# A graph layer on one core: the values' projection put behind the key-value sums, norms moved to ScalarE, tiles packed to 125 columns

## The chip, the cores and the metric

The kernel runs on one core of a Trainium2 chip. A core has TensorE (matrix products; PE in the profile, PEld for the loading of its stationary operands), VectorE (DVE), ScalarE (ACT), GpSimd (POOL) and SyncE (SP), which here only issues transfers. Times are device microseconds (us) of a whole execution; a kernel's time is the median of its runs. The profile is of one execution, and its times count from the start of the profiled span.

## The reference

A graph of N = 3125 nodes with C = 256 features and 53125 edges (src, dst, weight), sorted by dst. All in f32:

```
xn  = layernorm(x)
Q, K = elu(xn Wq) + 1, elu(xn Wk) + 1      # 8 heads of 32
v   = (xn Wv) / N
KV  = sum over nodes of K (x) v, per head  # 32x32 each
Z   = 1 / (Q . sum of K + 1e-6), per node and head
msg = layernorm((Q KV Z N) Wm) g1 + b1
msg = layernorm(relu([xn, msg] W1) W2) g2 + b2
x   = x + (segment sum of weight * xn[src] by dst) W.T + b + xn + msg
x   = x + two best of 16 experts of layernorm(x), softmax weights
```

The attention is linear, so its sums over all nodes (KV and the sum of K) must be complete before the first query can be used.

## The kernel before

The nodes lie in 25 tiles of V = 125 rows; in SBUF a tile is padded to P = 128. Four stages follow each other.

**Projections and sums (0 to 111 us).** For each tile t, `normed` makes xn (L416, on VectorE), turns it with two transposes (L428) and copies the turned tile into xnT (L429). `projected` multiplies by W and Wk at once (L437, 512 columns) and by Wv (L439, 256 columns); ScalarE makes exp and relu of the keys (L441, L443), copies v with its factor 1/N (L447), copies y = xn W.T (L448) and replaces x by x + xn (L454); VectorE ends the keys (L445, k_sb). `summed`, issued one tile later, adds K^T v and, with a column of ones behind each half of v, K^T 1 into one PSUM bank pkv (L461, 129 columns for each of two halves). The means, variances and the chain of 13 small operations that finds 1/sqrt (`moments`, `rsqrt`) are made for BATCHES of tiles; AHEAD says at which tile a batch's statistics are asked for.

**The edge lists.** In the same time VectorE makes the edge lists in pieces (`windows`): a search for the row of dst in which each group of 5 nodes starts (cmp_h, row_f, row_i, L248 to L253), five gathers of those rows on GpSimd (L257), in them the place of the first edge (cmp_r and its sum, L267 to L272), five gathers of windows of 128 edges (L273), and then keys and weights from these (src_f, L286, and the operations over 640 elements that follow). The table first_d of the starts is stored on SP's queue after the last of them. LISTS says at which tile how many pieces are asked for. From tile HOT = 18 on, two `adjacency` blocks go along with each tile: VectorE spells out one-hot matrices (L335, L340), TensorE multiplies them (L355), ScalarE copies, SP stores.

**Groups of queries (122 to 556 us).** `asked` makes Q of a group of 3 or 4 tiles (L477, L483), the denominators (L489, one product of all columns with the sum of K spread over each head's 32 columns), and their reciprocals on all 128 partitions (L493 to L495). `mixer` multiplies by kvw, which is KV times Wm (L641), and does the two-layer network (L662, L673). The next group's `asked` is interleaved with it, and adjacencies and first messages (L625) with both, by the numbers in `groups`. Between the sums and the first group stand the mask that cuts KV to its heads, its transposes (L533), its product with Wm (L538), sixteen one-column products for a bias (L544), and a loop for edges that fit no window, which these inputs never enter (L559).

**Messages to 708 us, then the experts.** All messages are products of 128 x 128 adjacency blocks with y of a tile.

The instructions of each engine stand in an order that a planner has chosen when the program was built, from its own costs and from "issue after" notes; on an engine they run strictly in that order, so an instruction that waits holds up all behind it.

Of the kernel before, what the change touches and what calls it, by code (L numbers as in the profile page):

```python
# [17 lines left out]
N = 3125  # L18
# [35 lines left out]
BATCHES = ((0, 2), (2, 5), (5, 12), (12, 25))  # L54

LISTS = {1: 1, 6: 1, 7: 2, 8: 2, 14: 1, 15: 1, 16: 1}
AHEAD = {1: (2, 5), 2: (5, 9), 3: (9, 12), 4: (12, 15), 6: (15, 17), 9: (17, 21), 10: (21, 25)}
HOT = 18
# [4 lines left out]
def tile_gps_layer(ctx: ExitStack, tc: tile.TileContext, a: dict, out: bass.AP):  # L63
# [7 lines left out]
    y_d = dram.tile([NT * P, C], F32, name="y_d")  # L71
# [12 lines left out]
    def rsqrt(var, n, with_last=False):  # L84

        v = small.tile([P, 13], F32, name="rs_v")[:, :n]
        hv = small.tile([P, 13], F32, name="rs_h")[:, :n]
        bits = small.tile([P, 13], I32, name="rs_b")[:, :n]
        y = small.tile([P, 13], F32, name="rs_y")[:, :n]
        s = small.tile([P, 13], F32, name="rs_s")[:, :n]  # L90
# [10 lines left out]
    def stats(mv, src):  # L101
        st = small.tile([P, 6], F32, name="bn_st")
        nc.vector.bn_stats(st, src)
        return nc.vector.bn_aggr(mv, st)
# [58 lines left out]
    wcat = w_mix.tile([128, 2, 3 * C], F32, name="wcat")  # L163
    load_x(nc.sync, *LOADS[0])
    nc.scalar.dma_start(dst_0, a["dst"].rearrange("(p j) -> p j", p=V)[:, 0:1])
    for i, name in enumerate(("gnn_WT", "Wk", "Wv")):
        nc.scalar.dma_start(wcat[:, :, i * C : (i + 1) * C], a[name].rearrange("(k p) o -> p k o", p=128))
    load_x(nc.sync, *LOADS[1])
    wq = w_mix.tile([128, 2, C], F32, name="wq")
    wm = w_mix.tile([128, 2, C], F32, name="wm")  # L170
    w1 = w_mix.tile([128, 4, F], F32, name="w1")
    w2 = w_mix.tile([128, 4, C], F32, name="w2")

    def load_later(t):

        if t in (0, 1):
            load_x(nc.sync, *LOADS[4 + t])
        if t in (11, 13, 15, 17):
            w, name = ((wm, "Wm"), (wq, "Wq"), (w1, "W1"), (w2, "W2"))[(t - 11) // 2]
            nc.sync.dma_start(w, a[name].rearrange("(k p) o -> p k o", p=128))  # L180
        if t == 19:


            nc.sync.dma_start(out[N:, :].rearrange("(p r) (k c) -> p (r k) c", r=2, k=2),
                              ones[:, None, :].to_broadcast([LANES, 4, P]))
# [11 lines left out]
    xnT = w_mix.tile([128, 2, NT * P], F32, name="xnT")  # L197
# [11 lines left out]
    kv_bd = w_mix.tile([128, 2, 128], F32, name="kv_bd")  # L209
# [9 lines left out]
    def bank_a(of=4 * P):  # L219
        return adj_ps.tile([128, 512], F32, name="pa")[:, :of].rearrange("p (i e) -> p i e", e=of // 4)  # L220

# [7 lines left out]
    def windows():  # L229
# [11 lines left out]
        busy(16)  # L241
# [138 lines left out]
    pkv = kv_ps.tile([128, 2, 129], F32, name="pkv")  # L380
# [3 lines left out]
    v_ring = [w_mix.tile([P, 2, 129], F32, name=f"v_sb{i}") for i in range(3)]  # L384
    for v_sb in v_ring:
        nc.vector.memset(v_sb[:, :, 128:129], 1.0)
# [22 lines left out]
    def normed(t):  # L409

        nonlocal rstd, r0
        for t0, t1 in BATCHES:
            if t == t0:
                rstd, r0 = ready.pop(t0), t0
        xn = work.tile([P, C], F32, name="xn", bufs=4)
        ins = nc.vector.tensor_scalar(xn, x_all[:, t, :], mv[:, t, 0:1], rstd[:, t - r0 : t - r0 + 1],  # L416
                                      op0=ALU.subtract, op1=ALU.mult)
        with tc.issue_after(ins.ins):
            for batch in BATCHES:
                if t == batch[0]:  # L420
                    factors(*batch, rstd)
# [4 lines left out]
        ptr = a_ps.tile([128, 2, P], F32, name="tok", bufs=3)  # L426
        for k in range(2):
            nc.tensor.transpose(ptr[:, k, :], xn[:, k * 128 : (k + 1) * 128], ident)  # L428
        nc.scalar.copy(xnT[:, :, t * P : (t + 1) * P], ptr)  # L429

    def projected(t):

        cols = slice(t * P, (t + 1) * P)
        pyk = a_ps.tile([P, 2 * C], F32, name="big")
        pv = a_ps.tile([P, C], F32, name="tok", bufs=3)
        for k in range(2):
            nc.tensor.matmul(pyk, lhsT=xnT[:, k, cols], rhs=wcat[:, k, : 2 * C], start=(k == 0), stop=(k == 1))  # L437
        for k in range(2):
            last = nc.tensor.matmul(pv, lhsT=xnT[:, k, cols], rhs=wcat[:, k, 2 * C :], start=(k == 0), stop=(k == 1))  # L439
        ek = work.tile([P, C], F32, name="ek", bufs=2)  # L440
        nc.scalar.activation(ek, pyk[:, C:], AF.Exp)  # L441
        k_sb = work.tile([P, C], F32, name="k_sb")
# [3 lines left out]
        v_sb = v_ring[t % 3]  # L446
        v_copy = nc.scalar.activation(v_sb[:, :, :128], pv.rearrange("p (c v) -> p c v", c=2), AF.Copy, scale=1.0 / N)  # L447
        nc.scalar.copy(y_of(t), pyk[:, :C])  # L448
        stored = nc.sync.dma_start(y_d[t * P : (t + 1) * P, :], y_of(t))
# [3 lines left out]
        with tc.issue_after(v_copy.ins):  # L453
            nc.scalar.activation(x_all[:, t, :], x_all[:, t, :], AF.Identity, scale=by[:, t : t + 1],  # L454
                                 bias=less[:, t : t + 1])
        return last, k_sb, v_sb

    def summed(t, k_sb, v_sb):
        for c in range(2):

            nc.tensor.matmul(pkv[:, c, :], lhsT=k_sb[:V, c * 128 : (c + 1) * 128], rhs=v_sb[:V, c, :],  # L461
                             start=(t == 0 and c == 0), stop=(t == NT - 1), skip_group_check=True)

    groups = ((4, 5, 0), (4, 23, 5), (4, 23, 7), (4, 23, 7), (3, 23, 7), (3, 23, 7), (3, 23, 2))
# [3 lines left out]
    def asked(t0, nt):  # L468

        w = nt * P  # L470
        c0 = t0 * P
        qT = mix.tile([128, 2, GROUP * P], F32, name="qT")
        asked_for.append(qT)
        for c in range(2):
# [9 lines left out]
            yield  # L484

# [5 lines left out]
        for part in (slice(0, 2 * P), slice(2 * P, w)):  # L491
# [6 lines left out]
    queries = [asked(sum(g[0] for g in groups[:i]), g[0]) for i, g in enumerate(groups)]  # L498
    rstd, r0 = None, 0
    kept = None  # L500
    normed(0)
    for t in range(NT):
# [8 lines left out]
        if t + 1 < NT:  # L511
            normed(t + 1)
# [13 lines left out]
    nc.vector.tensor_tensor(ksum, same_head[:, None, :].to_broadcast(shape), pkv[:, :, 128:129].to_broadcast(shape),  # L526
                            op=ALU.mult)
    nc.vector.tensor_tensor(kv_bd, same_head[:, None, :].to_broadcast(shape), pkv[:, :, :128], op=ALU.mult)
    for _ in range(2):
        next(queries[0])  # L530
    ptr = a_ps.tile([128, 2, 128], F32, name="tok", bufs=3)
    for c in range(2):
        nc.tensor.transpose(ptr[:, c, :], kv_bd[:, c, :], ident)  # L533
    kvT = work.tile([128, 2, 128], F32, name="msgT", bufs=1)
    nc.scalar.copy(kvT, ptr)
    for c in range(2):
        pw = a_ps.tile([P, C], F32, name="tok", bufs=3)
# [3 lines left out]
    pb1 = a_ps.tile([P, C], F32, name="tok", bufs=3)[:, :4]  # L541
# [17 lines left out]
    with tc.If(n_loops > 0):  # L559
        with tc.For_i(0, n_loops, 1) as it:  # L560
# [20 lines left out]
            nc.vector.scalar_tensor_tensor(t_d, t_d, float(P), p_d, op0=ALU.mult, op1=ALU.add)  # L581
# [9 lines left out]
            for t in range(NT):  # L591
                one = sel.tile([V, P], F32, name="l_one")
                nc.vector.tensor_scalar(one, iota_p[:V, :], p_s, took, op0=ALU.is_equal, op1=ALU.mult)
                pg = a_ps.tile([P, C], F32, name="tok", bufs=3)
# [7 lines left out]
    b_ps = ps.enter_context(tc.tile_pool(name="b_ps", bufs=1, space=PSUM))  # L602

# [9 lines left out]
    def messages(part, t, n, alone=False):  # L613
# [3 lines left out]
        if alone:  # L617
            pb = bank_a(2 * C)[:P].rearrange("p (a b) c -> p a (b c)", a=2)
        else:
            pb = b_ps.tile([P, 2, C], F32, name="pb")  # L620
        for i in range(n):
            rows = neighbours(part, t + i)
            for k in range(t0, t1):

                nc.tensor.matmul(pb[:, i, :], lhsT=rows[:, k - t0, :], rhs=y_of(k),  # L625
                                 start=(k == t0 and i == 0), stop=(k == t1 - 1), skip_group_check=True)
        nc.vector.tensor_tensor(x_all[:, t : t + n, :], x_all[:, t : t + n, :], pb[:, :n, :], op=ALU.add)  # L627
# [3 lines left out]
    def mixer(t0, nt, qT, following):  # L631

        w = nt * P
        c0 = t0 * P
        mv = small.tile([P, GROUP, 2], F32, name="mv_m")
        mw = mix.tile([P, GROUP, C], F32, name="mw")
# [655 lines left out]
```

## Time and profile before

| | |
|---|---|
| median of 3 runs | 1038.11 us (1036.63 to 1038.35) |
| the profiled execution | 1038.03 us, its span 1036.2 us |
| TensorE busy | 1007.1 us (97%), 6006 instructions |
| VectorE busy | 655.3 us (63%) |
| ScalarE, GpSimd busy | 263.9 us, 216.1 us |
| sum of tile 9 starts | 48.30 us |
| last sum ends, first group starts, second group starts | 110.9, 121.81, 152.86 us |
| last gather of edge windows issued, followed by the next waiting transfer | 34.18, 42.14 us |

In a line of the timeline stand: start, duration, engine, line, operation, output and inputs, tile, how many instructions were merged, and in brackets the idle time before it with what ended it. A product in f32 is two instructions, each of which runs over all columns. In a line of the stretches stand the stretch, its length, busy time and number of instructions of each engine, the granted clock of TensorE (1.00 is full speed), the share of the transfer engines in use and GB/s. A group's line has the busy time and the mean duration of one, then the engine's idle time before them and what ended it.

### The profile page before, as it was taken

How to read it: one execution, taken by the hardware profiler on the slowest of the kernel's cores; microseconds unless marked ns; L12 is line 12 of the kernel's file. 1: busy time of each engine (PE TensorE's matmuls, PEld its weight loads, DVE VectorE, ACT ScalarE, POOL GpSimd, SP SyncE). 2: the span in 40 equal slices, each digit the busy share in tenths (PEclk: the TensorE clock that was granted, in tenths of full speed). 3: DMA queues.
4: the chain of work that ended last, by engine and by line, in shares of the span. 5: the costliest groups of instructions: out<-in, count | busy, mean ns of one | idle time of the engine just before them, and what ended most of it. 6: DMA issues, size and time to landing. Idle time of an engine off the chain costs nothing.

```text
span 1036.2 us, 16279 instructions
## 1 busy us (share of the span) xinstructions
PE 1007.1 (97%) x6006; PEld 809.3 (78%) x6006; DVE 655.3 (63%) x1750; ACT 263.9 (25%) x577; POOL 216.1 (21%) x200
## 2 busy tenths in 40 slices
PE   7999999999999999999999999999999999999995
PEld 5667666686786887887877888887888888888884
DVE  8968699889787897956598148786932222222221
ACT  3666424323323233222141000103111111111110
POOL 3420100023100000000000001014445444545442
PEclk9999999999999999999999999999999999999998
DMA  6444104343344344553354455565757757667662
GB/s 214 95 131 145 53 31 167 128 140 136 122 137 138 133 162 133 175 181 143 140 182 155 159 167 166 183 194 179 209 155 226 240 170 234 199 202 225 206 189 26
DMA packets 70374, 165.09 MB, mean 159 GB/s; under 512 B 11091, under 2 KB 29934, under 8 KB 66314
## 3 DMA queue, kind: packets, MB, share of 16 engines
q1 hardware_dynamic: 53816, 138.10, 38.9%
q0 software_dynamic: 15520, 25.04, 10.7%
q8 instruction: 50, 0.82, 0.3%
q10 hardware_dynamic: 946, 0.79, 0.2%
q14 instruction: 42, 0.34, 0.1%
HBM read 105.85 MB, written 58.00 MB: 158 GB/s over the span
## 4 chain that ended last, share of the span: by engine, by line
PE 71%; DVE 10%; issue 1%; POOL 0%; ACT 0%; POOLq 0%; DVEq 0%; ACTq 0%
PE ph L1001 18%; PE pb L625 13%; PE po L1027 10%; PE po L738 8%; PE pa L355 6%; PE big L662 6%; PE tok L673 3%; DVE wone L340 2%; PE ptr L987 1%; PE pa L625 1%; PE big L477 1%; DVE one L335 1%; PE ph L799 1%; DVE wone L350 1%; PE big L489 1%
## 5 line engine op out<-in xcount | busy, mean ns | idle before, releaser
L1001 PE MATMUL ph<-xTb,wt 128*128 128x256 f32 (+2 forms) x992 | 204.5, 355 | 0.8 <-issue 0.8
L1001 PEld LDWEIGHTS ph<-xTb,wt 128*128 128x128 f32 x992 | 171.5, 190 | 24.9 <-ACT xTb L990 4.5
L625 PE MATMUL pb<-y_early,nbr 128*128 128x256 f32 x736 | 170.7, 382 | 0.4 <-DVE x_all L627 0.4
L340 DVE TENSOR_TENSOR wone<-one,wgts 128x1536 bf16<-128x1536 bf16 x150 | 140.6, 949 | 27.0 <-PE pa L355 26.8
L625 PEld LDWEIGHTS pb<-y_early,nbr 128*128 128x128 f32 x736 | 135.4, 190 | 17.2 <-DVE x_all L627 1.0
L355 PEld LDWEIGHTS <-one 128*128 128x128 bf16 x1875 | 117.3, 97 | 39.1 <-issue 19.1
L358 ACT COPY adj<-pa 128x512 f32<-128x512 f32 (+1 forms) x157 | 91.8, 586 | 194.2 <-PE pa L355 156.4
L355 PE MATMUL pa<-wone,one 128*128 128x128 bf16 x1875 | 130.3, 218 | 2.3 <-DVE wone L340 0.9
L1008 DVE TENSOR_TENSOR hid<-hid,ph 128x512 f32<-128x512 f32 (+2 forms) x62 | 38.3, 618 | 145.7 <-PE ph L1001 135.4
L1027 PE MATMUL po<-wt,hid 128*128 128x256 f32 (+1 forms) x456 | 115.2, 385 | 0.8 <-DVE yb L1030 0.7
L738 PE MATMUL po<-y_late,nbr 128*128 128x256 f32 x450 | 102.3, 381 | 0.5 <-DVE x_all L627 0.5
L335 DVE TENSOR_TENSOR one<-iota,keys 128x1024 bf16<-128x1024 bf16 x150 | 100.8, 692 | 0.7 <-POOL wgts L317 0.7
L1031 POOL DMA_INDIRECT out<-yb,to_l x45 | 70.9, 1576 | 114.4 <-DVE yb L1030 63.4
L1027 PEld LDWEIGHTS po<-wt,hid 128*128 128x128 f32 (+1 forms) x456 | 79.1, 184 | 17.6 <-DVE yb L1030 5.5
L738 PEld LDWEIGHTS po<-y_late,nbr 128*128 128x128 f32 x450 | 83.4, 190 | 11.2 <-DVE x_all L627 0.9
L1007 ACT ACTIVATE hid<-ph 128x512 f32<-128x512 f32 (+2 forms) x62 | 33.6, 542 | 208.4 <-PE ph L1001 204.4
L1030 DVE TENSOR_SCALAR yb<-po,sh 128x256 f32<-128x256 f32 (+1 forms) x57 | 27.5, 482 | 57.3 <-PE po L1027 54.9
L751 POOL IOTA rev<- 125x16 f32 x1 | 0.2, 156 | 296.5 <-PE pb L625 296.5
L700 POOL TENSOR_TENSOR x_all<-x_all,cb 128x256 f32<-128x256 f32 x25 | 25.7, 1050 | 148.2 <-DVE x_all L627 140.5
L627 DVE TENSOR_TENSOR x_all<-x_all,pb 128x512 f32<-128x512 f32 (+1 forms) x37 | 24.3, 655 | 41.8 <-PE pb L625 41.8
L662 PE MATMUL big<-xnT,w 128*128 128x512 f32 (+1 forms) x112 | 49.8, 556 | 0.0
L437 PE MATMUL big<-wcat,xnT 128*128 128x512 f32 x100 | 49.0, 612 | 0.0
(285 smaller groups left out, 1202.5 us busy)
## 6 DMA issues: line engine op xcount, KB each, us to landing
wt<-in_w SPq DMA_DIRECT2D x28, 1536.0 KB
adj_d<-adj SPq DMA_DIRECT2D x156, 256.0 KB
nbr<-adj_d SPq DMA_DIRECT2D x25, 576.0 KB
nbr<-adj_d SPq DMA_DIRECT2D x50, 256.0 KB
nbr<-adj_d SPq DMA_DIRECT2D x25, 512.0 KB
wt<-in_w POOLq DMA_DIRECT2D x3, 1536.0 KB
out<-x_all SPq DMA_DIRECT2D x25, 125.0 KB
x_all<-in_x SPq DMA_DIRECT2D x4, 640.0 KB
```

The lines of the kernel that those rows point to most:

```text
L335: nc.vector.tensor_tensor(one.rearrange("p b h e j -> p (b h) e j"), iota_2[:, None, :, :].to_broadcast(shape), ql.rearrange("p b h j -> p ...
L340: nc.vector.tensor_tensor(wone, one[:, :, 1:2, :, :].to_broadcast(shape), w[:, :, :, None, :].to_broadcast(shape), op=ALU.mult)
L355: nc.tensor.matmul(pa[:, j, :], lhsT=one[:, j // 2, 0, :, j % 2], rhs=wone[:, j // 2, i, :, j % 2], start=(i == 0), stop=(i == 2))
L358: copied = nc.scalar.copy(rows[:, :n, :], pa[:, :n, :])
L437: nc.tensor.matmul(pyk, lhsT=xnT[:, k, cols], rhs=wcat[:, k, : 2 * C], start=(k == 0), stop=(k == 1))
L625: nc.tensor.matmul(pb[:, i, :], lhsT=rows[:, k - t0, :], rhs=y_of(k), start=(k == t0 and i == 0), stop=(k == t1 - 1), skip_group_check=True)
L662: nc.tensor.matmul(ph[:, :w], lhsT=w1[:, k, j * 128 : (j + 1) * 128], rhs=rhs, start=(k == 0), stop=(k == 3))
L738: last = nc.tensor.matmul(pg, lhsT=rows[:, k - t0, :], rhs=y_of(k), start=(k == t0), stop=(k == t1 - 1))
L1001: last = nc.tensor.matmul(p[:, m, :w], lhsT=self.wt[:, i, k * F + at : k * F + at + 128], rhs=self.xT[:, k, :w], start=(k == 0), stop=(k = ...
L1008: self.units = nc.vector.tensor_tensor(hid, hid, pre[1], op=ALU.mult)
L1027: last = nc.tensor.matmul(po[:n_r, r, :], lhsT=self.hid[:, k, r * LANES : r * LANES + n_r], rhs=self.wt[:, 2, k * C : (k + 1) * C], start= ...
L1031: made.append(nc.gpsimd.indirect_dma_start(out=out[:, :], out_offset=bass.IndirectOffsetOnAxis(ap=at, axis=0), in_=yb[:n_r, r, :], in_offs ...
```

## The change

- **Values.** v is not projected per tile. The sums are taken of K with xn itself (257 columns with a column of ones behind xn, one PSUM bank for each half), and the 256 x 256 result is turned (four transposes) and multiplied by Wv once, behind the last sum. Wv is loaded at tile 9 of the projections.
- **Norms.** From tile 5 (ON_ACT) xn is made by ScalarE as x * rstd + less, not by VectorE. xn is kept in a ring of six tiles whose ones are written by GpSimd. `turned` is split from `normed`, which now runs two tiles ahead.
- **Pieces and chains.** BATCHES, LISTS and AHEAD have other numbers: one first chain of five tiles, the pieces of the edge lists from tile 7 to 17. The adjacencies start at tile 19; group 0 takes 7 of them in place of 5.
- **Reciprocals.** In groups 0 and 1 the denominators are made compactly: one number per node and head (products with four columns), a small reciprocal, then a copy that spreads it and products with the identity that turn it.
- **Packing.** xnT, qT, mT and the stored y have 125 columns or rows per tile, so a group has 500 or 375 columns in place of 512 or 384.
- **Loads.** W and Wk are loaded on SP's queue behind x in place of ScalarE's; the warm-up has 24 products in place of 16; the PSUM tiles "tok" get a third bank in a pool of its own once the sums are done.

```diff
-BATCHES = ((0, 2), (2, 5), (5, 12), (12, 25))
-LISTS = {1: 1, 6: 1, 7: 2, 8: 2, 14: 1, 15: 1, 16: 1}
-AHEAD = {1: (2, 5), 2: (5, 9), 3: (9, 12), 4: (12, 15), 6: (15, 17), 9: (17, 21), 10: (21, 25)}
-HOT = 18
+BATCHES = ((0, 5), (5, 9), (9, 15), (15, 25))
+LISTS = {1: 1, 7: 1, 8: 1, 9: 2, 10: 1, 15: 1, 16: 1, 17: 1}
+AHEAD = {2: (5, 7), 3: (7, 9), 5: (9, 11), 6: (11, 13), 7: (13, 15), 11: (15, 18), 12: (18, 21), 13: (21, 25)}
+ON_ACT = 5
+HOT = 19
...
-    for i, name in enumerate(("gnn_WT", "Wk", "Wv")):
-        nc.scalar.dma_start(wcat[:, :, i * C : (i + 1) * C], a[name].rearrange("(k p) o -> p k o", p=128))
     load_x(nc.sync, *LOADS[1])
+    for i, name in enumerate(("gnn_WT", "Wk")):
+        nc.sync.dma_start(wcat[:, :, i * C : (i + 1) * C], a[name].rearrange("(k p) o -> p k o", p=128))
...
-        busy(16)
+        busy(24)
...
+        xn = xn_ring[t % 6]
+        by_t = rstd[:, t - r0 : t - r0 + 1]
+        if t >= ON_ACT:
+            ins = nc.scalar.activation(xn[:, :C], x_all[:, t, :], AF.Identity, scale=by_t, bias=less[:, t : t + 1])
+        else:
+            ins = nc.vector.tensor_scalar(xn[:, :C], x_all[:, t, :], mv[:, t, 0:1], by_t,
+                                          op0=ALU.subtract, op1=ALU.mult)
...
-        pv = a_ps.tile([P, C], F32, name="tok", bufs=3)
...
-        for k in range(2):
-            last = nc.tensor.matmul(pv, lhsT=xnT[:, k, cols], rhs=wcat[:, k, 2 * C :], start=(k == 0), stop=(k == 1))
...
-        v_copy = nc.scalar.activation(v_sb[:, :, :128], pv.rearrange("p (c v) -> p c v", c=2), AF.Copy, scale=1.0 / N)
...
+            nc.tensor.matmul(pkv[:, c, : C + 1], lhsT=k_sb[:V, c * 128 : (c + 1) * 128], rhs=xn[:V, :],
+                             start=(t == 0), stop=(t == NT - 1))
...
-    groups = ((4, 5, 0), (4, 23, 5), (4, 23, 7), (4, 23, 7), (3, 23, 7), (3, 23, 7), (3, 23, 2))
+    groups = ((4, 7, 0), (4, 23, 5), (4, 23, 7), (4, 23, 7), (3, 23, 7), (3, 23, 7), (3, 23, 2))
...
+        if compact:
+            pn = tok([V, GROUP, H])
+            for i in range(nt):
+                for c in range(2):
+                    nc.tensor.matmul(pn[:, i, c * 4 : c * 4 + 4], lhsT=qT[:, c, i * V : (i + 1) * V],
+                                     rhs=ksum[:, c, 0:128:D], start=True, stop=True)
+            zn = small.tile([V, GROUP, H], F32, name="zn")
+            nc.vector.tensor_scalar(zn[:, :nt], pn[:, :nt], 1.0 / N, ATT_EPS / N, op0=ALU.mult, op1=ALU.add)
+            nc.vector.reciprocal(zn[:, :nt], zn[:, :nt])
+            yield
+            for c in range(2):
+                p = a_ps.tile([128, 512], F32, name="big")
+                zw = mix.tile([128, GROUP * P], F32, name="eq")[:V, : nt * 128].rearrange("p (i h d) -> p i h d", h=4, d=D)
+                nc.scalar.copy(zw, zn[:, :nt, 4 * c : 4 * c + 4, None].to_broadcast([V, nt, 4, D]))
+                for i in range(nt):
+                    nc.tensor.matmul(p[:, i * V : (i + 1) * V],
+                                     lhsT=zw[:, i].rearrange("p h d -> p (h d)"),
+                                     rhs=ident[:V, :V], start=True, stop=True)
+                nc.vector.tensor_tensor(qT[:, c, :w], qT[:, c, :w], p[:, :w], op=ALU.mult)
+            yield
+            return
...
-    queries = [asked(sum(g[0] for g in groups[:i]), g[0]) for i, g in enumerate(groups)]
+    queries = [asked(sum(g[0] for g in groups[:i]), g[0], i < 2) for i, g in enumerate(groups)]
...
-            normed(t + 1)
+            turned(t + 1)
+        if t + 2 < NT:
+            normed(t + 2)
...
-    nc.vector.tensor_tensor(kv_bd, same_head[:, None, :].to_broadcast(shape), pkv[:, :, :128], op=ALU.mult)
+    k_by = work.tile([128, 2, C], F32, name="k_by", bufs=1)
+    nc.scalar.activation(k_by, pkv[:, :, :C], AF.Copy, scale=1.0 / N)
+    turned_k = a_ps.tile([128, 512], F32, name="big")
+    for c in range(2):
+        for k in range(2):
+            nc.tensor.transpose(turned_k[:, (2 * k + c) * 128 : (2 * k + c + 1) * 128],
+                                k_by[:, c, k * 128 : (k + 1) * 128], ident)
+    by_k = work.tile([128, 2, 2, 128], F32, name="by_k", bufs=1)
+    nc.scalar.copy(by_k.rearrange("p k c n -> p (k c n)"), turned_k)
+    pvk = tok([128, 2, 128])
+    for c in range(2):
+        for k in range(2):
+            nc.tensor.matmul(pvk[:, c, :], lhsT=wv[:, k, c * 128 : (c + 1) * 128], rhs=by_k[:, k, c, :],
+                             start=(k == 0), stop=(k == 1))
+    kvT = work.tile([128, 2, 128], F32, name="msgT", bufs=1)
+    nc.vector.tensor_tensor(kvT, same_head[:, None, :].to_broadcast(shape), pvk, op=ALU.mult)
```

## The prediction

> **What bounds the kernel now.** I read the shares of busy time first, then busy time by stretches, then the instructions of TensorE, VectorE, ScalarE and GpSimd in order of time over the first 155 us.
>
> ```profile
> PE 1007.1 (97%) x6006; PEld 809.3 (78%) x6006; DVE 655.3 (63%) x1750; ACT 263.9 (25%) x577; POOL 216.1 (21%) x200
> ...
> 20.00:40.00 20.00, 20.00 (x86) 13.33 (x85) 19.10 (x88) 12.36 (x38) 9.29 (x11) 1.00 0.60 130
> 40.00:60.00 20.00, 20.00 (x86) 13.33 (x85) 15.15 (x30) 11.98 (x36) 2.35 (x3) 1.00 0.33 97
> ...
> 122.00:153.00 31.00, 29.76 (x129) 18.53 (x129) 27.62 (x57) 9.88 (x23) 1.23 (x2) 1.00 0.11 39
> ```
>
> TensorE is the bound of the whole. But from 20 to 40 us VectorE is busy for 19.10 of 20 us beside it, and in the first group of queries (122 to 153) for 27.62 of 31: these are the two places where VectorE takes over as soon as TensorE has less to do. TensorE's order of one tile of projections:
>
> ```profile
> 45.05 0.61 PE L461 MATMUL pkv<-v_sb,k_sb 125*128 125x129 f32 x4
> 45.50 0.39 PE L428 MATMUL tok<-ident,xn 128*128 128x128 f32 x2
> 45.72 1.88 PE L437 MATMUL big<-wcat,xnT 128*128 128x512 f32 x4
> 47.44 1.03 PE L439 MATMUL tok<-wcat,xnT 128*128 128x256 f32 x4
> 48.30 0.61 PE L461 MATMUL pkv<-v_sb,k_sb 125*128 125x129 f32 x4
> ```
>
> From start to start: sum 0.45, transposes 0.22, W and Wk 1.72, Wv 0.86; a period of 3.25 us with no gap. The line at 48.30 is the sum of tile 9. The last sum ends at 110.9 and the first group's first product (L641) starts at 121.81, group 1's at 152.86.
>
> ```profile
> 12.88 1.41 POOL L257 DMA_INDIRECT rows<-in_dst,row_i  x1 [9.49 <-DVE rs_s L97]
> ...
> 32.67 1.20 POOL L273 DMA_INDIRECT win<-in_edges,start_i  x1 [0.31 <-DVE start_f L271]
> 34.18 1.21 POOL L273 DMA_INDIRECT win<-in_edges,start_i  x1 [0.30 <-issue]
> ...
> 42.14 0.73 POOL L280 DMA_DIRECT2D gate_w<-in_gate_w  x1 [0.87 <-DMA win<-in_edges,start_i]
> ```
>
> ```profile
> 42.67 0.41 DVE L416 TENSOR_SCALAR xn<-x_all,mv,rs_y 128x256 f32<-128x256 f32 x1 [0.41 <-PE tok L428]
> 43.05 0.60 DVE L286 CAST src_f<-win 125x640 f32<-125x640 int32 x1
> ```
>
> The edge lists hang on gathers. The last of the five edge windows is issued at 34.18, and what waits for it goes on at 42.14: 7.9 us. In the trace's packet records a window's packets otherwise follow some 3 us behind their issue and take 1.75 us (4.9 us in all); but here the 625 four-byte packets of first_d (33.70 to 36.32) lie in between, and after them even 1 KB packets take up to 3.6 us. Before the change nobody suffers: src_f (L286) comes at 43.05, behind other work.
>
> **The change, part by part.** (1) TensorE per tile. L439 goes (-0.86), the sum takes 257 columns in place of 129 (four passes of 257 by the 216 ns of a 256-column pass, 0.86 in place of 0.45), transposes and stationary operands of 125 columns change nothing to speak of. Period 2.79, and 4.17 in place of 4.68 where two adjacencies go along (1.4 for both). From the start of the sum of tile 9 to the end of the last sum: before 8 x 3.25 + 7 x 4.68 + 3.44 (two parts of Q) + 0.45 = 62.65 (trace: 62.6); after, with the hot stage from tile 19, 9 x 2.79 + 6 x 4.17 + 3.36 + 0.86 = 54.3.
>
> (2) When is the sum of tile 9? By TensorE alone some 4 us earlier than 48.30. VectorE decides, in its order as built. One first chain over five tiles puts three more statistics (0.40 each) ahead: the first xn starts at 8.94 in place of 7.74. The first product follows then, and the eight more warm-up products (16 instructions, 1.75 us) end at about 9.2, just under it; if the cover were gone they would cost up to 1.75, but VectorE is what is late. Four xn come ahead of the row search (+0.93), so row_i is ready at 14.4 (12.37). The five row gathers are issued from 14.9 on and land, 4.9 us behind the issue as before and 2.0 apart, at 19.8, 21.8, 23.8, 25.8 and 27.8. cmp_r(0) now stands right behind the first k_sb (17.0) and waits 2.4 us; behind it in VectorE's queue stand the rsqrt chains and the k_sb of tiles 1 to 4, and TensorE's sums wait for these. The later cmp_r wait little. start_i of the last window is ready at 30.2, its gather is issued at 31.65 (POOL takes 1.5 per gather), 2.5 earlier than before. VectorE reaches src_f at 34.2, and in its queue k_sb(5) stands behind src_f.
>
> So T, the landing of the last window, counts now. Bounds: 4.9 us after the issue, 36.5; or 7.9, 39.5. first_d's store again falls 0.5 us ahead of the last issue (it follows the same start_i by the same 1.0), so the near row is the one with the pause: T = 39.5. From src_f to the end of k_sb(9) VectorE has: src_f 0.52, fifteen passes over 640 elements (0.42 to 0.93 from start to start in the trace, 9.2 in all), five k_sb at 0.33, small operations of a chain 1.4: 12.8. Sum of tile 9 at T + 12.9 = 52.4 (+4.1). The idle wait of 5 us ahead of it will halve TensorE's clock (in the trace a gap of 2.57 us made the next W/Wk product 3.27 us instead of 1.88, and the step lost 1.75); four tiles at 2.79 and 1.75 are 12.9, so it just hides under VectorE's 12.9. End of the sums: 52.4 + 54.3 = 106.7 against 110.9: **-4.2**.
>
> (3) Layer norms on ScalarE. ScalarE per tile loses v's copy (0.39, issued every 0.28) and gains an activation with two pointers. The rows:
>
> ```profile
> 48.50 0.39 ACT L447 ACTIVATE v_sb<-tok 128x256 f32<-128x256 f32 x1
> 48.78 0.59 ACT L454 ACTIVATE x_all<-x_all,less,by 128x256 f32<-128x256 f32 x1
> ```
>
> The Trainium skill (ScalarE: Activation LUTs, "Rules for kernel authors") says to do additions and multiplications on VectorE, not ScalarE, and speaks against this: 0.59 here against 0.41 for L416. Its own price (186 ns + 0.833 per element, 93 for each pointer: 585) agrees with the 590. As ScalarE then has four copies or exponents and two such activations, 4 x 0.38 + 2 x 0.59 = 2.7 by whole durations, 4 x 0.28 + 2 x 0.49 = 2.1 by starts, it stays under the period of 2.79 by either. I take the starts: no cost; VectorE is freed of 20 x 0.31 = 6.2 us, most of it after 40 us where it isn't the bound.
>
> (4) The tail behind the sums. kv's path becomes: copy, four transposes (0.43), copy, eight 128-column passes (0.86), in place of two transposes (0.22): +1.07. The compact reciprocal of group 0 replaces four 512-column passes (1.72) by 16 products of 4 columns and 16 of 125. For the tiny ones:
>
> ```profile
> 115.54 1.84 PE L544 MATMUL tok<-b,w 128*128 128x1 f32 x16
> 117.24 2.82 PE L477 MATMUL big<-xnT,wq 128*128 128x512 f32 x6
> ```
>
> Sixteen one-column products took 117.24 - 115.54 = 1.70. The skill (TensorE: Matmul & The Clock Gate, "Wait — 56ns, not 53.3ns?") puts the floor between two starts at about 25 ns however few the columns: 0.4 for sixteen. The row is of the same type with its own weight load for each, so I take 1.70; with the floor it would be 1.3 less per group, 2.6 in all. The 16 of 125 columns are 1.75 (109 each). Compact: 1.70 + 1.75 - 1.72 = +1.73. With Q1 shorter by 0.08 the tail has **+2.7**; its waits (k_by and by_k on ScalarE, zn and its reciprocal on VectorE) lie under Q1, L544 and two adjacencies, about 6 us of products; uncovered they would cost some 2.
>
> (5) Group 0: two more adjacencies (moved here from the sums, 1.4), the compact reciprocal of group 1 +1.73, 500 columns for 512 -0.75: **+2.4**. VectorE loses eight reciprocals of 1.64 (L494) in groups 0 and 1 and gets tiny ones: 12 us less. TensorE's idle time that this can give back is 1.24 in 122 to 153 (31 - 29.76) and about as much in group 1; I take half: **-1.2**, bounds 0 and -2.5.
>
> (6) From group 1 on the order of every engine is practically the old one; 512 to 500 and 384 to 375 columns (L662, L477, L489) save **-2.2**. The messages' operands get 125 columns but the moving side keeps 256, and the experts are untouched: 0. Bounds for weights read at a 500-byte pitch, of which no row tells: 0 to +1.
>
> Sum: -4.2 + 2.7 + 2.4 - 1.2 - 2.2 = -2.5, against the profiled execution's 1038.03 (span 1036.2 and 1.8 around it; the median of the runs is 1038.11, so nothing to correct): **1035.5 us**.
>
> **Rivals.** (a) The pause after first_d doesn't come, or VectorE reaches src_f with all windows there: T = 36.5 gives 1032.5, T = 34.2 gives 1030.2. For it: three of the five gathers in the trace had no pause. Against it: the order store, gather is the same. (b) Beyond that the gathers cost nothing and the groups' idle time goes too, TensorE's work alone decides: its sum is -21.6 (L439) + 10.7 (sums) + 1.07 + 3.5 - 2.2 and -0.4 of smaller transposes = -8.9, with the stalls of 100 to 175 us -10.5: 1027.5. Against it: VectorE's 95%. (c) Slower: the windows land later still. From 39.5 every us of T is one us of the end; at T = 42 the change brings nothing, from 44 on it is slower by over 0.2%. If row_i slips by 2 us more (the loads of x and of the weights, now both on SP's queue, stand ahead of it) and the pause takes 9 us, T = 45.5 and the end is 1041.5. For it: 42.1 was the landing before, with an earlier row_i. (d) The projection moved behind the sums gives back its gain there: the tail's waits uncovered (+2) and each tiny product as long as its weight load (190 ns on the page, 16 x 0.19 = 3.04 in place of 1.70, +2.7 in two groups): 1040.2. Against it: L544.
>
> **How the numbers follow.** My forecast 0.40 (own range 1033.5 to 1038.5), (a) 0.25, (b) 0.12, (c) 0.13, (d) 0.10. The range for 8 in 10 runs from (b), 1027.5, to (c), 1041.5. A difference of 0.2%, 2.1 us, is about what a measurement of this kernel can tell from none. Faster by more: just over half of the forecast's 0.40, and (a) and (b): 0.58. Within: 0.17. Slower: 0.25.
>
> **What would show it.** In the changed profile: sums of 257 columns every 2.79 us between tile 10 and 18; VectorE idle ahead of the first cmp_r for about 2.4 us and ahead of src_f for about 5, both put down to a DMA; TensorE idle there and its clock lower about 40 us; the last sum's end at 106.7; the first group's start at about 120.3 and group 1's at about 153.2 (before 152.86: up to here nothing is won, and half of the -1.2 lies behind); from there on the old order, shorter by 2.8. I am wrong if src_f doesn't wait, if ScalarE ends TensorE's waits in the sums, or if group 0 takes more than 35 us.

## The result

The changed kernel takes 1049.26 us (median of 4 runs, 1048.78 to 1050.82) against 1037.68 for the kernel before: a ratio of 1.0114, 95% interval 1.0103 to 1.0126. It is 11.6 us slower; the forecast was 1035.5, range 1027.5 to 1041.5. The profiled execution took 1048.78, its span 1047.2.

The share of busy time and the stretches of the changed kernel (columns as before: stretch, length, PE, PEld, DVE, ACT, POOL, TensorE's clock, transfers, GB/s):

```profile
PE 1005.8 (96%) x5988; PEld 804.2 (77%) x5988; DVE 631.0 (60%) x1719; ACT 265.1 (25%) x569; POOL 216.8 (21%) x206
...
20.00:40.00 20.00, 13.36 (x38) 7.76 (x38) 13.07 (x69) 8.82 (x24) 10.75 (x12) 0.74 0.52 107
40.00:60.00 20.00, 14.62 (x45) 8.42 (x44) 12.99 (x37) 9.78 (x28) 2.45 (x4) 0.91 0.31 70
...
122.00:153.00 31.00, 29.32 (x159) 20.23 (x159) 20.14 (x48) 10.43 (x23) 4.94 (x4) 0.95 0.07 27
```

TensorE has less to do, as forecast. But from 20 to 60 us, where it had been busy all 40, it is now busy for 28, at a mean clock of 0.74 and 0.91, and VectorE is busy for only 26 of the 40. Neither engine is the bound there: both wait. TensorE's and VectorE's instructions in order of time say for what:

```profile
17.34 1.10 PE L475 MATMUL pkv<-xn,k_sb 125*128 125x257 f32 x4 [3.13 <-DVE rs_y L100]
...
27.02 2.05 PE L475 MATMUL pkv<-xn,k_sb 125*128 125x257 f32 x4 [6.64 <-DVE less L403]
...
46.86 2.05 PE L475 MATMUL pkv<-xn,k_sb 125*128 125x257 f32 x4 [5.38 <-DVE mv L106]
...
59.78 1.03 PE L475 MATMUL pkv<-xn,k_sb 125*128 125x257 f32 x4
```

```profile
24.94 0.61 DVE L278 TENSOR_TENSOR cmp_r<-rows,thr 125x425 bf16<-125x425 int32 x1 [7.67 <-DMA rows<-in_dst,row_i]
...
26.45 0.42 DVE L462 SCALAR_TENSOR_TENSOR k_sb<-ek,k_sb 125x256 f32<-125x256 f32 x1
...
45.80 0.58 DVE L297 CAST src_f<-win 125x640 f32<-125x640 int32 x1 [6.71 <-issue]
46.30 0.41 DVE L462 SCALAR_TENSOR_TENSOR k_sb<-ek,k_sb 125x256 f32<-125x256 f32 x1
```

The first line is the sum of tile 0, the last that of tile 9. Between them a sum (L475) waits for VectorE two times, that of tile 1 at 27.02 and that of tile 5 at 46.86. Both times the keys (k_sb) follow within 0.5 to 1.5 us an operation on the edge lists that had stood before them in VectorE's queue and waited for a gather: cmp_r for the rows (7.67 us), src_f for the windows (6.71). The instruction that the first kind of line names as releaser (less, mv) is only the last VectorE operation before the keys; the cause is one step further back. After both long waits the sum takes 2.05 us where it takes 1.03 in a row: half clock.

GpSimd's queue and SP's queue show the gathers and the loads, the changed kernel first:

```profile
14.88 1.41 POOL L268 DMA_INDIRECT rows<-in_dst,row_i  x1 [11.30 <-DVE bn_st L105]
...
36.33 1.21 POOL L284 DMA_INDIRECT win<-in_edges,start_i  x1 [0.30 <-DVE bn_st L105]
...
44.03 0.74 POOL L291 DMA_DIRECT2D gate_w<-in_gate_w  x1 [3.15 <-DMA win<-in_edges,start_i]
```

```profile
15.20 0.28 SPq L464 DMA_DIRECT2D y_d<-y_early  x1
15.52 0.45 SPq L163 DMA_DIRECT2D x_all<-in_x  x1
```

The same load in the kernel before:

```profile
19.02 0.33 SPq L449 DMA_DIRECT2D y_d<-y_early  x1
19.39 0.43 SPq L161 DMA_DIRECT2D x_all<-in_x  x1
```

The rows were issued at 14.88, as forecast, but landed 10 us later, not 4.9. The load of x's last five tiles is issued behind the store of y of tile 1; that store comes 3.8 us earlier than before, so the load goes out at 15.52, beside the row gathers. By stages (us; the stages after the second group's start have the old order):

| | before | forecast | after |
|---|---|---|---|
| first cmp_r starts | 23.37 | 19.8 | 24.94 |
| src_f starts | 43.05 | 39.5 | 45.80 |
| sum of tile 9 starts | 48.30 | 52.4 | 59.78 |
| last sum ends | 110.9 | 106.7 | 116.1 |
| first group starts | 121.81 | 120.3 | 131.41 |
| second group starts | 152.86 | 153.2 | 165.57 |
| from there to the span's end | 883.3 | 880.5 | 881.6 |

### The profile page after: what moved, and what is told of

It reads as the page before. It is cut to its first block, busy times and chain, and to the rows that moved or that the text cites. A ratio compares the mean times of both kernels' runs of the same rounds, so it can differ in the third digit from the quotient of the medians.

```text
span 1047.2 us, 16206 instructions
## 1 busy us (share of the span) xinstructions
PE 1005.8 (96%) x5988; PEld 804.2 (77%) x5988; DVE 631.0 (60%) x1719; ACT 265.1 (25%) x569; POOL 216.8 (21%) x206
## 3 DMA queue, kind: packets, MB, share of 16 engines
q0 software_dynamic: 15520, 25.04, 10.7%
## 4 chain that ended last, share of the span: by engine, by line
PE 70%; DVE 10%; issue 1%; ACT 0%; POOL 0%; POOLq 0%; ACTq 0%; DVEq 0%
PE ph L1053 18%; PE pb L677 13%; PE po L1079 10%; PE po L790 8%; PE pa L366 6%; PE big L714 5%; PE tok L725 3%; DVE wone L351 2%; PE ptr L1039 1%; PE pa L677 1%; PE big L491 1%; DVE one L346 1%; DVE wone L361 1%; PE ph L851 1%; PE big L525 1%
## 5 line engine op out<-in xcount | busy, mean ns | idle before, releaser
L677 PE MATMUL pb<-y_early,nbr 125*125 125x256 f32 x736 | 170.6, 382 | 0.4 <-DVE x_all L679 0.4
L677 PEld LDWEIGHTS pb<-y_early,nbr 125*125 125x125 f32 x736 | 133.7, 188 | 18.7 <-DVE x_all L679 1.0
L790 PE MATMUL po<-y_late,nbr 125*125 125x256 f32 x450 | 102.3, 381 | 0.5 <-DVE x_all L679 0.5
L790 PEld LDWEIGHTS po<-y_late,nbr 125*125 125x125 f32 x450 | 82.3, 188 | 12.2 <-DVE x_all L679 0.9
L456 PE MATMUL big<-wcat,xnT 128*125 128x512 f32 x100 | 50.0, 622 | 0.0
L679 DVE TENSOR_TENSOR x_all<-x_all,pb 125x512 f32<-125x512 f32 (+1 forms) x37 | 24.3, 658 | 41.7 <-PE pb L677 41.7
L714 PE MATMUL big<-xnT,w 128*128 128x500 f32 (+1 forms) x112 | 48.6, 548 | 0.0
```

What stands on the lines that cost most here:

```text
L456: last = nc.tensor.matmul(pyk, lhsT=xnT[:, k, cols], rhs=wcat[:, k, :], start=(k == 0), stop=(k == 1))
L677: nc.tensor.matmul(pb[:V, i, :], lhsT=rows[:V, k - t0, :V], rhs=y_of(k)[:V], start=(k == t0 and i == 0), stop=(k == t1 - 1), skip_group_ch ...
L714: nc.tensor.matmul(ph[:, :w], lhsT=w1[:, k, j * 128 : (j + 1) * 128], rhs=rhs, start=(k == 0), stop=(k == 3))
L790: last = nc.tensor.matmul(pg, lhsT=rows[:V, k - t0, :V], rhs=y_of(k)[:V], start=(k == t0), stop=(k == t1 - 1))
```

## The experiments

The theory from the changed profile: late transfers hold VectorE's queue, and with it the keys. The rivals: VectorE's order alone is the cause (where the pieces of the edge lists stand), or the loss lies in the tail with the compact reciprocals. "k_sb of tile n" is the keys' last operation.

**The loads of x.** x1_early keeps every engine's order and sends SP's loads of tiles 15 to 24 out right behind those of 5 to 14.

```diff
-        if t in (0, 1):
+        if t in ():
             load_x(nc.sync, *LOADS[4 + t])
...
-    for batch in LOADS[2:4]:
+    for batch in LOADS[2:6]:
```

> The changed kernel, but the loads of x's tiles 15 to 24 go out right behind those of 5 to 14 (about 7 us) in place of behind the stores of y of tiles 0 and 1 (13.6 and 15.5 us); every engine's order is the same. Theory (transfers): with the faster second tile the last load started at 15.5 in place of 19.4 and shares the queues with the first row gather (issued at 14.9), so that VectorE's first cmp_r waits until 24.9. Then here cmp_r starts at 20 to 21, src_f about 4 us earlier than 45.8, and the time is 1044 to 1046. Rival (the order alone): the gathers are late because they are issued 2 us later and because VectorE's queue stands behind them; the loads don't matter, cmp_r still waits to 24 or 25, 1049.

Measured: 1043.99 us, ratio 1.0068 (1.0045 to 1.0090): 5.3 us less than the changed kernel. VectorE in order of time:

```profile
21.03 0.61 DVE L278 TENSOR_TENSOR cmp_r<-rows,thr 125x425 bf16<-125x425 int32 x1 [3.92 <-DMA rows<-in_dst,row_i]
...
40.40 0.59 DVE L297 CAST src_f<-win 125x640 f32<-125x640 int32 x1 [6.50 <-issue]
```

The rows come 3.9 us earlier, all else follows; that the loads don't matter is refuted. How much they cost is not the same in every profile. From the issue of the first row gather to the cmp_r that waits for it pass 7.3 to 11.1 us in the four profiles that have the loads where the changed kernel has them (it, and three of the runs below: x2, x4, x6), and 6.3 and 6.8 us in the two that have them early (x1, x3). The forecast's 4.9 came in none of these.

**The store of first_d.** x2_store makes it wait for src_f.

```diff
-        nc.sync.dma_start(first_d.rearrange("(i r) o -> r (i o)", r=V), start_i)
...
-        nc.vector.tensor_copy(src_f, win[:, :, :, 0])
+        copied = nc.vector.tensor_copy(src_f, win[:, :, :, 0])
+        stored = nc.sync.dma_start(first_d.rearrange("(i r) o -> r (i o)", r=V), start_i)
+        tc.add_manual_dep(stored.ins, copied.ins.name, SYNC, reason="behind the windows")
```

> The changed kernel, but the store of first_d (625 packets of four bytes) waits until src_f has read the windows. Theory (transfers): the pause between 38 and 44 us comes from this store; without it the last window lands some 4.9 us behind its issue at 36.3, src_f starts at 41 to 42 in place of 45.8, and the time is 1044.5 to 1046. Rival: the pause is that of the rows of b, gnn_b and g that GpSimd's queue fetches behind the windows, or the windows' own; then src_f stays at 45 to 46 and the time at 1049.

Measured: 1044.51 us, 1.0075 (1.0051 to 1.0100).

```profile
36.16 1.21 POOL L284 DMA_INDIRECT win<-in_edges,start_i  x1 [0.30 <-DVE bn_st L105]
...
41.23 0.70 DVE L296 CAST src_f<-win 125x640 f32<-125x640 int32 x1 [2.54 <-DMA win<-in_edges,start_i]
```

The last window was issued at 36.16 here and read at 41.23: 5.1 us, against 36.33 and 45.80, 9.5 us, with the store beside it. So the 625 packets of four bytes cost the windows some 4 us; the broadcast rows on GpSimd's queue were the same in both. The other profiles agree: the last window takes 9.0 to 10.7 us from its issue to src_f where the store goes out beside it (x1, x4, x6, x11, x13), and 5.5 where it doesn't (x3). A rival is that first_d, while it waits in SP's queue, also holds back the stores of y behind it. But in the packet records of x2 the packets of y run beside the last windows all the same, 37 to 61 of them starting in each us from 36 to 40.

> Both edits of the loads and of the first_d store. Theory (transfers): they add up, src_f at about 37, the sum of tile 9 at about 50 in place of 59.8, and the time is 1039.5 to 1042; what then stays against the kernel before is the tail and group 0. Rival (the order alone): 1048 to 1049.

Both edits together: 1039.87 us, 1.0022 (1.0015 to 1.0028). src_f at 37.51, sum of tile 9 at 51.28, last sum's end at 107.6, about what the forecast had for the changed kernel. But the end is 4.4 us above the forecast, 3.8 in the profiled execution: 0.9 of it lies ahead of the sums' end, 1.8 in the tail and group 0 (48.3, forecast 46.5) and 1.2 behind them.

**The reciprocals.** x4_plain calls `asked` with compact = False for all groups.

> The changed kernel with the reciprocals of groups 0 and 1 made as before (on all 128 partitions). In the changed profile the compact way took 1.67 + 3.04 us of products in the tail, where TensorE's clock fell to half, and 1.77 + 1.92 in group 0, in place of 1.72 each. Theory: 5.0 us of products fall away and about 1 us of VectorE's reciprocals shows again: 1045 to 1046. By the prediction's step (3.5 us of products against 1.2 of stalls): 1047. Rival: the compact way is paid back by VectorE, 1049 or more.

Measured: 1046.05 us, 1.0089 (1.0058 to 1.0120). The row gather happened to land earlier in its profile (22.14), so the stage alone is read: from the last sum's end to the second group 47.7 us, against 49.5 in the changed kernel and 42.0 before. Of the 7.5 that were lost there the compact way holds 1.8; 1.1 of this is a spell of half clock, since in x2 and x3, where the clock stays whole there, the same products take 48.4 and 48.3. Of what is left 1.4 are the two moved adjacencies; and TensorE waits longer than before, now with the old reciprocals:

```profile
127.19 1.10 PE L714 MATMUL big<-xnT,w 128*128 128x500 f32 x2 [1.21 <-ACT qT L495]
...
134.18 1.10 PE L525 MATMUL big<-qT,ksum 128*128 128x500 f32 x2 [0.80 <-ACT eq L529]
136.03 1.94 PE L714 MATMUL big<-xnT,w 128*128 128x500 f32 x4 [0.74 <-ACT eq L529]
138.91 0.43 PE L705 MATMUL tok<-ident,mw 125*128 125x125 f32 x2 [0.94 <-DVE mw L701]
...
142.20 1.08 PE L714 MATMUL big<-mT,w 128*128 128x500 f32 x2 [0.93 <-ACT mT L706]
```

With 0.43 more ahead of an adjacency these are 5.1 us, where the kernel before waited 2.2 (0.95, 0.81, 0.43). The order of the tail and of group 0 is another one, and it fits worse. The last 1.4 of the 7.5 are not traced; the longer path of kv had been put at 1.07.

**The order on VectorE.** x5_held leaves loads and stores as they are and only orders each piece of the edge lists behind the newest k_sb:

```diff
             for _ in range(LISTS.get(t, 0)):
-                next(pieces, None)
+                with tc.issue_after(keyed[-1].ins) if keyed else nullcontext():
+                    next(pieces, None)
...
-        nc.vector.scalar_tensor_tensor(k_sb, ek, 1.0, k_sb, op0=ALU.min, op1=ALU.add)
+        keyed.append(nc.vector.scalar_tensor_tensor(k_sb, ek, 1.0, k_sb, op0=ALU.min, op1=ALU.add))
```

> The changed kernel with its loads and the first_d store untouched; only each piece of the edge lists is ordered behind the newest k_sb on VectorE, so that cmp_r stands behind the k_sb of tile 4 and src_f behind that of tile 14 (in the changed kernel behind tiles 0 and 4). Theory (a late gather costs because the wait stands in VectorE's queue ahead of the keys): the gathers land as late as before but nothing waits, the sum of tile 9 starts at 45 to 47 in place of 59.8, the last sum ends at 101 to 104, and the time is 1036 to 1040; if the weights then come too late for tile 19, some us more. Rival (the transfers themselves, or TensorE's clock, hold the sums): 1047 or more.

Measured: 1037.25 us, 0.9995 (0.9981 to 1.0010), 12 us less than the changed kernel, with every late transfer still there. The sum of tile 9 starts at 45.69. src_f no longer waits, and no key stands behind a waiting gather; what is new is a wait of the first adjacency for its weights, since the pieces now come late:

```profile
52.53 0.62 DVE L297 CAST src_f<-win 125x640 f32<-125x640 int32 x1
74.50 0.69 DVE L346 TENSOR_TENSOR one<-iota,keys 128x1024 bf16<-128x1024 bf16 x1 [4.63 <-POOL wgts L328]
```

So the late transfers cost what they did only because VectorE's queue put them ahead of the keys. Which part of the change did that? x6_dve makes all norms on VectorE again:

```diff
-ON_ACT = 5
+ON_ACT = 25
...
-            if t == 0:
-                factors(*BATCHES[0], rstd)
+            for batch in BATCHES:
+                if t == batch[0] and t < ON_ACT:
+                    factors(*batch, rstd)
```

> The changed kernel with all layer norms on VectorE again (the factors of every batch made behind its first norm). The planner then puts cmp_r behind the k_sb of tile 2 and src_f behind that of tile 10. Theory (order): the second wait, for the windows, falls mostly away, the first costs less; VectorE has 6 us more to do: 1041 to 1045. Rival (norms on ScalarE relieve VectorE, as the change has it): 1050 or more.

Measured: 1036.93 us, 0.9996 (0.9984 to 1.0009): with this one part undone all of the loss is gone, more than I had expected. The waits that are left:

```profile
25.14 0.61 DVE L278 TENSOR_TENSOR cmp_r<-rows,thr 125x425 bf16<-125x425 int32 x1 [1.40 <-DMA rows<-in_dst,row_i]
48.41 0.59 DVE L297 CAST src_f<-win 125x640 f32<-125x640 int32 x1 [0.84 <-issue]
```

The rows come as late as before (25.14), but cmp_r stands behind the k_sb of tile 2, and src_f behind that of tile 10. And the converse, x13_act_alone: the kernel before with that part alone.

```diff
+        by_t = rstd[:, t - r0 : t - r0 + 1]
+        for batch in BATCHES:
+            if t == batch[0] and t >= 5:
+                factors(*batch, rstd)
+        if t >= 5:
+            ins = nc.scalar.activation(xn, x_all[:, t, :], AF.Identity, scale=by_t, bias=less[:, t : t + 1])
+        else:
+            ins = nc.vector.tensor_scalar(xn, x_all[:, t, :], mv[:, t, 0:1], by_t, op0=ALU.subtract, op1=ALU.mult)
```

> The kernel before, with one part of the change alone: layer norms from tile 5 on ScalarE. In the order as built src_f then stands behind the k_sb of tile 5 in place of tile 8, and the first cmp_r behind tile 1 in place of 2. Theory (order): the windows land at about 42 as before, the k_sb of tile 6 is needed at 38.5, so the sums lose about 3 to 5 us: 1040 to 1043. Rival (VectorE is relieved of 6 us in its fullest stretch and the sums are bound by TensorE anyway): 1036 to 1038.

Measured: 1047.43 us, 1.0109 (1.0091 to 1.0126). VectorE, and then TensorE:

```profile
32.36 0.41 DVE L451 SCALAR_TENSOR_TENSOR k_sb<-ek,k_sb 128x256 f32<-128x256 f32 x1
41.65 0.59 DVE L286 CAST src_f<-win 125x640 f32<-125x640 int32 x1 [8.80 <-DMA gate_b<-in_gate_b]
46.00 0.42 DVE L451 SCALAR_TENSOR_TENSOR k_sb<-ek,k_sb 128x256 f32<-128x256 f32 x1
```

```profile
46.56 1.20 PE L467 MATMUL pkv<-v_sb,k_sb 125*128 125x129 f32 x4 [7.90 <-DVE rs_s L96]
```

The windows land at about the old time (src_f reads them; the row names a load that was issued behind them on the same queue). src_f stands three keys earlier in the queue than before, waits 8.8 us, and the sums with it: nearly the loss of the whole change, from one of its parts. The size was beyond what I had expected (3 to 5): nothing covers the wait, and the operations behind src_f come in the keys' way too (the next key is 4.3 us behind it).

**What is left of the other parts.** x8_held_plain has the pieces behind the keys, both transfer edits and the old reciprocals; x9_held_one the same with compact reciprocals in group 1 alone (`i == 1`).

> The changed kernel with the x loads right behind each other, first_d behind src_f, the pieces behind the keys, and the reciprocals of groups 0 and 1 as before. Theory: the sums are bound by TensorE alone (sum of tile 9 at 44 to 46, last sum's end at 100 to 102), the tail and group 0 take about 47.7 as in the run without compact reciprocals (before: 42.0), later groups win about 2: 1032 to 1036, faster than both kernels. Rival: something else holds the sums or the weights come too late for tile 19: 1038 or more.

> As the run with the pieces behind the keys and both transfer edits, but with the compact reciprocals in group 1 alone, so that the tail has the old ones. Theory (the tail's products with four columns leave the array idle and the clock halves): without them in the tail the clock stays whole there and its 125-column products with the identity are gone: tail 11 to 12.5 in place of 15.4, but group 0 as in the changed kernel or up to 2 longer; 1 to 2 us less than with the reciprocals in both. Compared with both old (the run beside this): within 2.

Measured: x8 1033.41 us, 0.9953 (0.9936 to 0.9970); x9 1035.45, 0.9973 (0.9962 to 0.9985). The tail of x9 is 10.9 us, as long as before. From the last sum's end to the second group x8 takes 47.7 and x9 49.4. That isn't the price of the products alone: x9's profile has 3.4 us at half clock there (130.2 to 133.6), which by itself can be worth 1.7. What the compact way costs in group 1 with the clock whole is thus not shown; over all its runs x9 is 2.0 us slower than x8. x11_values has the moved projection and the packed tiles alone, all other numbers as before the change:

> The changed kernel with the values' projection behind the sums and the packed tiles alone: norms on VectorE, the numbers of the pieces, chains, warm-up, hot stage and group 0 as before, no compact reciprocals. src_f stands behind the k_sb of tile 8. Theory: the sums win about 6 to 9 us, the tail loses 1 to 4, later groups win 2: 1030 to 1034. Rival (the moved projection gives all back in the tail): 1037 or more.

Measured: 1035.65 us, 0.9988 (0.9981 to 0.9994). A gain, but of 1 us, between the theory's and the rival's. The last sum ends 3.5 us earlier (107.4), though src_f waits 3.6 here too: the last load of x goes out as late as before (19.93), but the last window is issued 2.2 us later than before (36.33), with the store of first_d beside it, and read at 47.01; the tail and group 0 take 46.4 in place of 42.0 and give more than this back; the later groups win the rest.

x10_best is x8 with the pieces asked for two to three tiles earlier; x12_dve_plain has the norms on VectorE, the two transfer edits and the old reciprocals, in the planner's own order.

```diff
-LISTS = {1: 1, 7: 1, 8: 1, 9: 2, 10: 1, 15: 1, 16: 1, 17: 1}
+LISTS = {1: 1, 5: 1, 6: 1, 7: 2, 8: 1, 12: 1, 13: 1, 14: 1}
```

> As the run with the pieces behind the keys and the old reciprocals, but the pieces asked for two to three tiles earlier, since there the first adjacency waited 4.6 us for its weights. Theory: these waits (2.4 us of TensorE) go and nothing new comes: 1030 to 1032.5. Rival: the windows' wait comes back into the keys' way: 1034 or more.

> The changed kernel with all norms on VectorE, the x loads right behind each other, first_d behind src_f and the old reciprocals; the order of the pieces is the planner's. Theory: 1037 with norms on VectorE alone, less about 2 for the reciprocals, less 1 to 2 for the first gather's wait (1.4) and the clock behind it: 1032 to 1035. Rival: 1036 or more.

Measured: x10 1031.38 us, 0.9952 (0.9935 to 0.9969); x12 1032.09, 0.9963 (0.9949 to 0.9977). Both are faster than either kernel. In x10 TensorE's wait for the first adjacency (2.0 us in x8) is gone, but 1.5 of waits for keys have come; its sums end at 101.1, those of x8 at 104.7, and 2.8 of this lie between the sums of tiles 0 and 1 (2.88 us apart, in x8 5.68, at half clock), which the edit doesn't touch. Why x10 is faster over all its runs is thus only half explained. x12 comes to the same with no norm on ScalarE: once the keys are free, the moved norms have brought nothing that a time shows (the two differ in the order of the pieces too).

## Why the prediction was wrong

**The step that failed is part (2), when the sum of tile 9 is.** Its mechanism was right: VectorE's queue, the wait of cmp_r, the wait of src_f, the keys behind them. The terms were too small. The row gathers were set at 4.9 us from issue to landing, as before; they took 10, because the second tile's y, and behind it the last load of x, come 3.8 us earlier, which the step had not followed (x1, with both late loads early: 3.9 us of it; the other 1.2 stay open). The windows were given 7.9 us with the store's pause, and took 9.4 (the pause itself was rightly read: x2). Together T was 45.7, not 39.5: 6.2 us. The sum of tile 9 came 14.0 behind it, not 12.9, and from there to the sums' end were 56.3, not 54.3: the count had left out the fifteen transposes of the edge lists (1.6 us) and waits of 1.0 for keys, and was some 0.6 too high elsewhere. That the same count met the old kernel's 62.6 us was luck, for these transposes lie in that stretch too (from 61.75 on). All this is 9.4 of the 13.3 us by which the profiled execution missed the sum. Rival (c) named this mechanism, with 0.13, and put the end at 1041.5 for T = 45.5, nearly the T that came. The 7 us beyond it are the longer way behind T (1.1 and 2.0) and what parts (4) to (6) missed. None of the three signs of being wrong came (src_f did wait, ScalarE did not end the sums' waits, group 0 took 34.2 us): they watched the mechanism, not the sizes.

**Part (3), norms on ScalarE, was costed at nothing; with the order that it brings it is the whole loss** (x6: -12.3, x13: +10.8). ScalarE did keep up: where nothing else held them, the sums came every 2.80 us. One norm took 0.59 to 0.63 us there, near the 585 ns that the step worked out from the Trainium skill (ScalarE: Activation LUTs, "What ACT_TABLE_LOAD costs"). x5 leaves the norms on ScalarE and loses nothing, so the price was not ScalarE's own. It was the order: with the norms off VectorE the planner put src_f behind the k_sb of tile 4, with them on it behind that of tile 10 (x6; tile 8 in the kernel before). The prediction had used the new order, but put its cost down to gathers and not to the part that made it.

**Part (4), the tail:** +4.4 in place of +2.7. The sixteen instructions of four columns (eight products, at two instructions each; L544 is eight products too) took 1.67 us, as the row had it (1.70), not the 0.4 that the prediction had weighed against it. What was missed is the clock: in the stretches

```profile
121.00:122.00 1.00, 1.00 (x8) 0.85 (x8) 0.41 (x2) 0.00 (x0) 0.00 (x0) 0.94 0.00 0
122.00:123.00 1.00, 1.00 (x4) 0.42 (x3) 0.13 (x1) 0.83 (x2) 0.00 (x0) 0.50 0.00 0
123.00:124.00 1.00, 1.00 (x5) 1.00 (x6) 0.00 (x0) 0.85 (x3) 0.00 (x0) 0.50 0.00 0
124.00:125.00 1.00, 1.00 (x7) 1.00 (x6) 0.06 (x1) 0.00 (x0) 0.00 (x0) 0.50 0.00 0
125.00:126.00 1.00, 1.00 (x10) 1.00 (x10) 0.62 (x1) 0.00 (x0) 0.00 (x0) 0.85 0.00 0
```

it is 0.50 behind the tiny products (119.71 to 121.4), and the 125-column products that follow took 3.04 us (122.84 to 125.88) where those of group 1 took 1.92. The tail takes 15.3 us with this spell (changed kernel, x1) and 14.2 with the same products at whole clock (x2, x3, x6): that is 1.1 of the 1.7 us by which the part was missed.

**Part (5), group 0:** +3.1 in place of +1.8. VectorE's freed time gave nothing back: TensorE's waits there were 1.52 us (1.24 before), for norms and adjacencies, not for reciprocals. **Part (6):** -1.7 in place of -2.8. **Part (1)** held: a period of 2.80 us.

## What to carry to other kernels

Moving work off an engine whose instructions run in a planned order changes that order: look at which waiting instruction moves ahead of which producer, and cost its wait as if nothing covered it, because a gather may land later than the planner counts on (in the orders that it chose here the waits were 7.7, 6.7 and 8.8 us). A faster first tile triggers the transfers that hang on it earlier; follow each of them to what else is in the queues at that time. An instruction that waits for a gather is best ordered behind the producers that the critical engine needs next.

## What was new about the hardware

- TensorE's clock is halved for whole stretches of 3.41 us, and this can happen though TensorE is hardly ever idle. In the fourteen profiles every spell at 0.50 between 8 us and the last product lasts 3.41 us or two or three times as long (in the changed kernel from 22.9 to 33.1, 46.8 to 50.2 and 121.9 to 125.3 us). What brings them can be estimated from the traces. Let a column of f32 take 0.84 ns (1.72 us for four instructions of 512) and one of bf16 0.45 ns (0.69 us for twelve of 128), and cut each profile into stretches of 3.41 us that begin where the spells begin. Of 4153 such stretches at whole clock 24 are followed by half clock. In these 24, columns pass for a share of at most 0.39 of the time; in all others for at least 0.38. Idle time alone doesn't tell them apart: ahead of five of the spells TensorE was idle for only 0.25 to 0.36 us.
- These five are the spells in the tail or in group 0, and all lie in profiles with compact reciprocals (the changed kernel, x1, x5, x6, x9); the stretches ahead of them have shares of 0.32 to 0.39, and sixteen instructions of four columns lie whole in each (in the changed kernel 119.71 to 121.38, in a stretch from 118.5 to 121.9). x2 and x3 have the same products and no spell: there a stretch ends in the middle of them, in the tail as in group 0, and no share falls below 0.44. In the seven profiles without them (before, x4, x8, x10, x11, x12, x13) the clock is 1.00 from the last sum to the second group, at shares of 0.39 and more. The sixteen one-column instructions (L544, 1.70 us) alone have never done it. So whether such products halve the clock depends on where the stretches happen to fall. The traces show this; no run was made for it alone. That one program has the spell in some executions and at different places fits the free-running window of which the Trainium skill tells (TensorE: Matmul & The Clock Gate, "What's actually happening"), and its 3413 ns are the length found here. But where the page's table names an idle window as what brings half clock, 0.25 us of idle in one were enough here.
- A store of 625 packets of four bytes delays the gather of windows that goes out beside it by some 4 us (5.1 and 5.5 us from issue to use without it in x2 and x3, 9.0 to 10.7 with it in six profiles), though it moves 2.5 KB.
